# Layer 1 attention: where the exponentials' sums are added, and when the product with ones follows

## The chip, the cores and the metric

The kernel runs on one core of a Trainium2 chip. The metric is the time of one execution on the device, in microseconds (us). All data is 32-bit floating point.

## The reference

Four batches of 1024 rows of x (512 features) pass through two layers of cross attention against a context of 1024 rows (384 features). Layer 0 has 16 heads of 64 features, a layer norm ahead of it and its own weights. Layer 1, the one that is changed, has 16 heads of 32 features. Cut to what matters:

```python
xn = x * rsqrt(mean(x * x) + EPS_RMS) * norm_w
q = (xn @ wq).reshape(B, 1024, 16, 32)
k, v = split((context @ wkv).reshape(B, 1024, 2, 16, 32))
q, k = rotate(q), rotate(k)                 # rotary embedding
q, k = q / norm(q), k / norm(k)             # over each head
attn = softmax(einsum("bqhd,bkhd->bhqk", q, k) * sqrt(32))
out = x + einsum("bhqk,bkhd->bqhd", attn, v).reshape(B, 1024, 512) @ wout
```

The softmax needs, for each query and head, the sum over 1024 keys of the exponentials. The kernel divides by it after the product with v.

## The kernel before

The batches run one after the other. Within a batch layer 0 goes through eight pairs of heads (`Attention0`), then layer 1 through two halves of its heads (`Attention1`): `half` 0 and 1, eight heads each, in two groups `g` of four heads.

A **block** of layer 1 is one `(half, g, qb)`: four heads (`j`) and 256 queries (`WQ`). A half has 8 blocks, all batches together 64. A block takes four **steps** `kk`, each of two tiles `c` of 128 keys, so a half has 32 steps, numbered `n` from 0, and `kk` is `n % 4`. One `step` issues:

- the scores: 8 calls (L577), keys in the partitions, queries along the row, into two tiles `s` of two PSUM banks each;
- two exponentials on ScalarE (L587) into `e`, which has one place for even and one for odd steps;
- `finish`: the division of an earlier block (`quotient`) if one is pending, then `product` of the step before: 8 calls (L616) that add v times the exponentials into the tile `av`, in bank f0;
- `fill`: as many queued items of other work as the remaining steps share out by their written costs;
- on VectorE two additions (L593), which put the step's two key tiles together into `both[:, kk]`, and for `kk` 1 and 2 one more (L597), which adds `both[:, kk]` to `both[:, 0]`.

After the last product of a block come the sums over the partitions: 4 calls with a tile of ones over `both[:, 0]` and 4 over `both[:, 3]` (L627), into the second half of `av`. Each call shows as two instructions in the profile. One ScalarE copy (L631) takes `av` to SBUF, and a step later VectorE forms the reciprocal (L634) and the product with it (L635), which gives the output tile `o`.

Within layer 1, all other PSUM tiles come from `bank`, which goes round f1, f2, f3; f0 is kept for `av`. In layer 0 it goes round f0 to f3. An item that begins a new tile takes the next bank and has to wait until the tile that had it before was read.

The queue of other work (`Units`) is a list written out by hand. In half 0 it holds chains of projections for q and k (`rotated_chains`: a projection, a square on ScalarE at L476 and three VectorE reads of the bank at L478 to L480, work on GpSimd at L485, L167, L489, and two chains later the transposes at L499), the values (`value_chains`), and four transposes for the norm (L245). The order within it, by `weave`, in short: projection of a chain, then the transposes of the chain two before. In half 1 it holds the output product of half 0 (`add_units`, evacuated by VectorE at L293) and the preparation of the next batch. In the last batch's half 1 (the *final* half) there are only output products; the blocks are sorted by `g`, so that a finished group of heads can be multiplied early. The output products of the last two groups are handed to the queue at fixed steps: 18, and 22, 26, 30.

At a batch's end `finish` and `quotient` are called at once, and layer 0 of the next batch begins. The tiles `both` and `rest` (which holds `avs` and half of the values) have the tag "big"; layer 0's `eT` take over these two buffers.

## Time and profile before

| | |
|---|---|
| median of 3 runs | 2955.73 us (2946.95 to 2957.67) |
| profiled execution, its own time | 2957.42 us |
| its span, first to last instruction | 2955.4 us |
| mean granted TensorE clock | 0.992 |
| TensorE (PE) busy | 2865.9 us, 97% |
| VectorE (DVE) busy | 2185.6 us, 74% |
| ScalarE (ACT) busy | 1436.6 us, 49% |
| GpSimd (POOL) busy | 935.9 us, 32% |
| L627, product with ones | 1024 instructions, 81.3 us busy |
| L593, additions of key tiles | 512, 701 ns each |
| L597, additions of steps | 128, 1248 ns each |
| L631, copy of `av` | 64, 587 ns each |
| L634 and L635, division | 64 each, 1748 and 498 ns |

How to read it: a share is busy time over the whole span, and busy times of PE overlap, because matmuls are pipelined: an instruction of 379 ns can follow another after 54. What an instruction adds to the path is read from the chain of waits, not from its duration. PEld is the loading of weights. In a group's line the number after the second bar is the idle time of the engine just before these instructions, and what ended it. A waiting time belongs to the last of several conditions. The timeline's columns are start, duration, engine, line, operation, tiles, shapes, and in brackets the idle time before.

### The profile page before, as it was taken

To read this page: it belongs to the slowest core of one execution; us is meant where nothing else is said; L and a number is where in the kernel's file an instruction comes from. 1 tells how busy PE (TensorE), PEld (TensorE's weight loads), DVE (VectorE), ACT (ScalarE), POOL (GpSimd) and SP (SyncE) were. 2 spreads that over 40 slices of the span, in tenths; PEclk is the share of its full clock that TensorE was granted. 3 is DMA by queue.
4 is the path that set the end of the run, shared out by engine and by line. 5 is a ranking of instruction groups with operands and counts; after the bars stand their busy time and mean duration, and the time that the engine had idled before them with its cause. 6 is when DMAs were issued, how large, how long until landed. Compare 5 with 4: busy or idle time off the path is not lost.

```text
span 2955.4 us, 66614 instructions
## 1 busy us (share of the span) xinstructions
PE 2865.9 (97%) x27336; PEld 1433.0 (48%) x27336; DVE 2185.6 (74%) x2952; ACT 1436.6 (49%) x2265; POOL 935.9 (32%) x776
## 2 busy tenths in 40 slices
PE   8999999999989999999998999999999999999998
PEld 4444445555444454555544444455554444445544
DVE  5677785877767778587776777868877677786787
ACT  4444444656434443466643444346664344444664
POOL 2343353320234335332023433534102343353310
PEclk9999999999999999999999999999999999999999
DMA  5878774010487877401048787730105887763000
GB/s 141 197 180 188 169 173 104 22 36 25 105 199 176 186 163 164 104 22 36 25 115 189 179 187 170 162 94 22 36 25 126 192 182 178 172 162 85 2 2 30
DMA packets 177552, 348.86 MB, mean 118 GB/s; under 512 B 37600, under 2 KB 93152, under 8 KB 177248
## 3 DMA queue, kind: packets, MB, share of 16 engines
q1 hardware_dynamic: 175920, 343.96, 49.5%
q8 instruction: 215, 3.52, 0.5%
q14 instruction: 89, 0.73, 0.1%
q10 hardware_dynamic: 1328, 0.66, 0.1%
HBM read 67.64 MB, written 8.39 MB: 26 GB/s over the span
## 4 chain that ended last, share of the span: by engine, by line
PE 80%; DVE 10%; SPq 4%; DMA 2%; issue 2%; ACT 1%; POOL 1%; DVEq 0%; ACTq 0%
PE s L365 15%; PE av L426 13%; PE po L163 10%; PE s L577 8%; PE pqT L163 7%; PE pv L163 7%; PE av L616 6%; PE pkT L163 6%; SPq L410 4%; PE q_p L163 3%; PE av L627 2%; DVE both L593 2%; DVE m L390 2%; PE k_p L163 1%; DMA wo<-in_Wo_dram 1%
## 5 line engine op out<-in xcount | busy, mean ns | idle before, releaser
L390 DVE TENSOR_REDUCE m<-s 128x1 f32<-128x1024 f32 x512 | 603.0, 1220 | 401.6 <-PE s L365 401.6
L587 ACT ACTIVATE e<-s 128x1024 f32<-128x1024 f32 x512 | 497.1, 1023 | 313.2 <-PE s L577 304.7
L391 ACT ACTIVATE e<-s,m 128x1024 f32<-128x1024 f32 x256 | 283.4, 1112 | 502.9 <-DVE m L390 240.7
L396 POOL TENSOR_SCALAR raw<-raw,li 128x1024 f32<-128x1024 f32 x256 | 286.4, 1119 | 734.2 <-DVE li L395 725.8
L365 PE MATMUL s<-qk 64*128 64x512 f32 x2048 | 518.1, 621 | 0.7 <-ACT qk L135 0.7
L391 ACT ACTIVATE raw<-s,m 128x1024 f32<-128x1024 f32 x256 | 285.9, 1117 | 470.0 <-DVE m L390 470.0
L426 PE MATMUL av<-eT,v 128*64 128x256 f32 x4096 | 470.4, 382 | 5.3 <-DMA eT<-e 2.3
L396 POOL TENSOR_SCALAR e<-e,li 128x1024 f32<-128x1024 f32 x256 | 286.3, 1119 | 493.8 <-DMA eT<-e 239.4
L593 DVE TENSOR_TENSOR both<-e 128x512 f32<-128x512 f32 x512 | 341.9, 701 | 116.1 <-ACT e L587 88.9
L426 PEld LDWEIGHTS av<-eT,v 128*64 128x64 f32 x4096 | 287.4, 137 | 225.2 <-issue 84.5
L365 PEld LDWEIGHTS s<-qk 64*128 64x128 f32 x2048 | 180.9, 188 | 283.9 <-issue 174.3
L577 PE MATMUL s<-q,k 32*128 32x256 f32 x4096 | 306.0, 401 | 5.9 <-ACT q L504 2.7
L399 DVE STREAM_TRANSPOSE e<-e 128x1024 f32<-128x1024 f32 x256 | 310.1, 1229 | 0.2
L399 DVE STREAM_TRANSPOSE e<-raw 128x1024 f32<-128x1024 f32 x256 | 310.0, 1229 | 0.0
L163 PE MATMUL po<-wo,vals 128*64 128x512 f32 x1024 | 242.7, 608 | 26.5 <-DMA wo<-in_Wo_dram 26.5
L577 PEld LDWEIGHTS s<-q,k 32*128 32x128 f32 x4096 | 192.2, 184 | 153.0 <-ACT e L587 72.1
L163 PE MATMUL pqT<-hT,w 128*64 128x512 f32 (+1 forms) x1216 | 240.7, 595 | 2.5 <-ACT hT L247 2.5
L293 DVE TENSOR_TENSOR x<-x,po 128x512 f32<-128x512 f32 x200 | 131.7, 679 | 112.2 <-PE po L163 112.2
L163 PEld LDWEIGHTS pv<-w,cT 128*64 128x64 f32 (+1 forms) x3360 | 170.3, 132 | 41.6 <-issue 34.8
L163 PE MATMUL pv<-w,cT 128*64 128x128 f32 (+1 forms) x3360 | 184.3, 274 | 0.7 <-ACT hT L247 0.7
L163 PE MATMUL pkT<-cT,w 128*64 128x512 f32 (+1 forms) x912 | 183.1, 597 | 0.0
L597 DVE TENSOR_TENSOR both<-both 128x1024 f32<-128x1024 f32 x128 | 159.7, 1248 | 4.4
(81 smaller groups left out, 2793.1 us busy)
## 6 DMA issues: line engine op xcount, KB each, us to landing
eT<-e SPq DMA_DIRECT2D x2048, 128.0 KB, 2.4
xr<-in_x_dram SPq DMA_DIRECT2D x32, 256.0 KB, 3.6
x<-in_x_dram SPq DMA_DIRECT2D x32, 256.0 KB, 4.6
wo<-in_Wo_dram SPq DMA_DIRECT2D x16, 512.0 KB, 4.4
out_dram<-x SPq DMA_DIRECT2D x32, 256.0 KB, 2.6
w<-in_Wq_dram SPq DMA_DIRECT2D x31, 256.0 KB, 3.1
c<-in_ctx_dram SPq DMA_DIRECT2D x32, 192.0 KB, 3.9
wkv<-in_wkv_dram SPq DMA_DIRECT2D x16, 384.0 KB, 3.4
```

The source lines that it names most:

```text
L163: nc.tensor.matmul(o[rr], lhsT[:, rr], rhs, start=start, stop=stop)
L365: nc.tensor.matmul(sc[j][:, kb * 512 : (kb + 1) * 512], pr["qT"][r[j], i * P : (i + 1) * P], pr["kT"][r[j], kb * 512 : (kb + 1) * 512], st ...
L390: nc.vector.tensor_reduce(m[:, j : j + 1], sc[j], AX.X, ALU.max, negate=True)
L391: nc.scalar.activation(e[j], sc[j].rearrange("p (g s) -> p g s", g=4), AF.Exp, bias=m[:, j : j + 1], accum_out=l[:, j : j + 1])
L396: nc.gpsimd.tensor_scalar(e[j], e[j], li[:, j : j + 1], HD0**-0.5, ALU.mult, ALU.mult)
L399: self.turn = [lambda j=j: nc.vector.transpose(self.e[:, :, i % BQ * 2 + j, :], e[j]) for j in range(2)]
L426: nc.tensor.matmul(av[r[j], :W].rearrange("p (t a i) -> p t a i", t=BQ, a=4), pr["v"][:, k, r[j]], eT[:, j, :, :, k * 32 : (k + 1) * 32], ...
L577: nc.tensor.matmul(sc[j // 2][:, j % 2, c, :], kT[rr, g, k * P : (k + 1) * P], qT[rr, g, qb * WQ : (qb + 1) * WQ], start=True, stop=True,)
L587: nc.scalar.activation(e, sc[u], AF.Exp, scale=float(np.sqrt(np.float32(HD1))))
L593: nc.vector.tensor_add(self.both[:, kk, 2 * u : 2 * u + 2, :], es[u][:, :, 0, :], es[u][:, :, 1, :])
L597: nc.vector.tensor_add(self.both[:, 0], self.both[:, 0], self.both[:, kk])
L616: nc.tensor.matmul(self.av[rr, 0, :], v[g][:, 2 * kk + c, rr], es[j // 2][:, j % 2, c, :], start=first and c == 0, stop=end and c == 1,)
```

## The change

`both` is used differently: places 0 and 1 are running sums `acc` for odd and even blocks, place 2 takes steps 1 and 2, place 3 the last step. The additions on VectorE stay as many. After a block's last product, the tile `av`, now half as wide, is copied at once; GpSimd adds `both[:, 3]` to `acc`; and the ones go over `acc` only, with 4 calls into a tile from `bank`, two steps after the last product with v (in the final half one step), ahead of that step's own product. A second copy takes the sums to SBUF, and the division follows one step later. At the end of batches 0 to 2 the three remaining calls of `finish` become items of the queue, ahead of the next batch's layer 0; in the last batch they follow at once. The output products of the last group are queued at steps 23, 27 and 31.

```diff
@@ Attention1.__init__
-            self.quotient = None
+            self.after = None
+            self.n = 0
+            self.hurry = False
@@ step
+            self.n += kk == 0
...
             self.finish()
-            self.last = (half, g, qb, kk, v, es, o)
+            self.last = (half, g, qb, kk, v, es, o, self.n % 2)
             self.u.fill(us)
+            acc, end = self.both[:, self.n % 2], self.both[:, 3]
+            into = acc if kk == 0 else end if kk == NT // 2 - 1 else self.both[:, 2]
             for u in range(2):
-                nc.vector.tensor_add(
-                    self.both[:, kk, 2 * u : 2 * u + 2, :], es[u][:, :, 0, :], es[u][:, :, 1, :]
-                )
+                nc.vector.tensor_add(into[:, 2 * u : 2 * u + 2, :], es[u][:, :, 0, :], es[u][:, :, 1, :])
             if 0 < kk < NT // 2 - 1:
-                nc.vector.tensor_add(self.both[:, 0], self.both[:, 0], self.both[:, kk])
+                nc.vector.tensor_add(acc, acc, into)
@@ finish
-            if self.quotient is not None:
-                self.quotient()
-                self.quotient = None
+            if self.after is not None:
+                self.after = self.after()
@@ product
-                self.av = ps_f.tile([P, 2, WQ], F32, tag="f0", name=f"av1_{n}")
+                self.av = ps_f.tile([P, WQ], F32, tag="f0", name=f"av1_{n}")
...
             if end:
-                for i in (0, NT // 2 - 1):
-                    for j in range(4):
-                        rr = slice(j * HD1, (j + 1) * HD1)
-                        nc.tensor.matmul(
-                            self.av[rr, 1, :], ones, self.both[:, i, j], start=i == 0, stop=i > 0
-                        )
-                s = self.avs[:, qb % 2]
-                nc.scalar.copy(s, self.av)
-                def divide(): ...
-                self.quotient = divide
+                s = self.avs[:, par]
+                nc.scalar.copy(s[:, 0, :], self.av)
+                acc = self.both[:, par]
+                nc.gpsimd.tensor_add(acc, acc, self.both[:, 3])
+                def sums():
+                    pp = bank(f"sum1_{n}")
+                    for j in range(4):
+                        rr = slice(j * HD1, (j + 1) * HD1)
+                        nc.tensor.matmul(pp[rr, :WQ], ones, acc[:, j], start=True, stop=True)
+                    nc.scalar.copy(s[:, 1, :], pp[:, :WQ])
+                    def divide(): ...          # the two VectorE instructions as before
+                    return divide
+                self.after = sums if self.hurry else lambda: sums
@@ the loop over batches
+            att1.hurry = final
...
-                    if final and n in (22, 26, 30):
-                        work.add(flat(adds[1][(n - 22) // 2 : (n - 18) // 2]))
+                    if final and n in (23, 27, 31):
+                        work.add(flat(adds[1][(n - 23) // 2 : (n - 19) // 2]))
...
         att1.finish()
-        att1.quotient()
+        if b == B - 1:
+            att1.finish()
+            att1.finish()
+        else:
+            work.add([(c, att1.finish) for c in (0.0, 0.25, 0.0)])
```

More of the change, by code (lines that the diff above doesn't have):

```diff
@@ L607, in product @@
         def product(self):
-            half, g, qb, kk, v, es, o = self.last
+            half, g, qb, kk, v, es, o, par = self.last
             n = f"{self.b}_{half}_{g}_{qb}"
             if kk == 0:
-                self.av = ps_f.tile([P, 2, WQ], F32, tag="f0", name=f"av1_{n}")
+                self.av = ps_f.tile([P, WQ], F32, tag="f0", name=f"av1_{n}")
             first, end = kk == 0, kk == NT // 2 - 1
@@ L616, in product @@
                     nc.tensor.matmul(
-                        self.av[rr, 0, :],
+                        self.av[rr, :],
                         v[g][:, 2 * kk + c, rr],
@@ L623, in product, with divide @@
             if end:
-                for i in (0, NT // 2 - 1):
+                s = self.avs[:, par]
[4 more added lines that the diff above has]
+                    pp = bank(f"sum1_{n}")
                     for j in range(4):
                         rr = slice(j * HD1, (j + 1) * HD1)
-                        nc.tensor.matmul(
-                            self.av[rr, 1, :], ones, self.both[:, i, j], start=i == 0, stop=i > 0
-                        )
-                s = self.avs[:, qb % 2]
-                nc.scalar.copy(s, self.av)
-                def divide():
-                    nc.vector.reciprocal(s[:, 1, :], s[:, 1, :])
-                    nc.vector.tensor_mul(o[g][:, qb * WQ : (qb + 1) * WQ], s[:, 0, :], s[:, 1, :])
-                self.quotient = divide
+                        nc.tensor.matmul(pp[rr, :WQ], ones, acc[:, j], start=True, stop=True)
+                    nc.scalar.copy(s[:, 1, :], pp[:, :WQ])
+                    def divide():
+                        nc.vector.reciprocal(s[:, 1, :], s[:, 1, :])
+                        nc.vector.tensor_mul(o[g][:, qb * WQ : (qb + 1) * WQ], s[:, 0, :], s[:, 1, :])
+                    return divide
+                self.after = sums if self.hurry else lambda: sums
             self.last = None
```

## The prediction

> **What bounds the kernel now.** I read the engine shares first, then the page's chain of waits by engine, then busy times by stretch.

> ```profile
> PE 2865.9 (97%) x27336; PEld 1433.0 (48%) x27336; DVE 2185.6 (74%) x2952; ACT 1436.6 (49%) x2265; POOL 935.9 (32%) x776
> ...
> PE 80%; DVE 10%; SPq 4%; DMA 2%; issue 2%; ACT 1%; POOL 1%; DVEq 0%; ACTq 0%
> ```

> TensorE is busy nearly throughout. For layer 1, the busy times of three stretches (PE, PEld, DVE, ACT, POOL): batch 0's half 0, its half 1, and the final half of batch 3.

> ```profile
> 494.00:627.00 133.00, 126.26 (x1918) 69.93 (x1920) 102.97 (x144) 83.08 (x111) 46.80 (x29) 0.99 0.06 17
> 627.00:754.00 127.00, 126.72 (x1786) 65.14 (x1788) 92.61 (x129) 81.14 (x99) 3.07 (x4) 1.00 0.11 35
> 2834.00:2941.00 107.00, 104.07 (x1359) 50.46 (x1352) 86.66 (x113) 66.05 (x72) 0.00 (x0) 1.00 0.03 9
> ```

> PE is the bound here too; half 0 loses 6.7 us of 133. The chain of waits inside half 1 shows one step and prices its parts:

> ```profile
> 642.93 1.08 PE s L577 x16
> 644.01 1.00 PE av L616 x16
> 645.01 0.86 PE av L627 x16
> 645.88 1.72 PE po L163 x16
> ```

> A step is scores (1.08), product with v (1.00), then queued work; on the first step of a block the 16 ones instructions (L627, two for each call) add 0.86 us, 53.75 ns each. Groups by form and PE's list of waits say what else L627 costs:

> ```profile
> L627 PE MATMUL av<-both,ones 128*32 128x256 f32 x1024 | 81.3, 382 | 15.4 <-DVE both L593 15.4
> ```
> ```profile
> PE av L627 <- DVE both L593: 15.4, 9, 2.2
> ...
> PE pth L245 <- DVE rot L480: 6.7, 4, 1.7
> ...
> PE q_t L499 <- POOL rot L489: 2.3, 4, 0.6
> ```

> The first wait is PE standing still for VectorE's last add. The second recurs once per batch and shows what a short bank rotation costs; the timeline of its place:

> ```profile
> 519.77 0.61 PE L163 MATMUL k_p<-wkv,cT 128*32 128x256 f32 x8
> ...
> 520.32 1.09 PE L245 MATMUL pth<-ident,xn 128*128 128x128 f32 x8
> ...
> 520.81 0.61 ACT L476 ACTIVATE rot<-k_p 128x512 f32<-128x512 f32 x1
> ...
> 521.58 0.68 DVE L478 TENSOR_TENSOR rot<-k_p,cos 128x512 f32<-128x512 f32 x1
> ...
> 522.51 0.42 DVE L480 TENSOR_TENSOR rot<-k_p,sin 128x256 f32<-128x256 f32 x1
> ...
> 523.07 0.63 PE L245 MATMUL pth<-ident,xn 128*128 128x128 f32 x4 [1.66 <-DVE rot L480]
> ```

> A projection ends at 520.3; two transposes take the other two banks; the third needs the projection's bank and waits until ScalarE's square and three VectorE reads are over, 2.7 us after the projection's end. At 586.8 the same series took 2.6 us, at 534.8 2.2 us.

> [...]

> ```profile
> 549.92 1.05 POOL L489 TENSOR_TENSOR rot<-rot,k_r 128x512 f32<-128x512 f32 x1
> ...
> 550.19 1.06 DVE L635 TENSOR_TENSOR o<-rest 128x256 f32<-128x256 f32 x1
> ```

> L635 takes 0.42 elsewhere. Beneath the power L167 (3.2 us) an L597 kept its 1.23[...]. [...] L478 above begins only after the square has ended. [...] L616 and L627 share 128*32 and follow without a gap; the moved ones stand right before a product, in the same mode.

> **The change, part by part.**

> *Removed.* Of each block's 8 ones calls 4 go: 8 instructions x 53.75 ns x 64 blocks = **27.5 us** of PE on the path. The wait for L593 loses its place: 15.4 less 0.3 of the very last block = **15.1 us**. Together 42.6.

> *GpSimd's add.* 128x1024 with two inputs is not in the trace; the nearest row is

> ```profile
> L282 POOL TENSOR_TENSOR x<-x,bo x32: 1260/1265/1274, 143.3 to 2407.2; 128x512 f32<-128x512 f32 x32
> ```

> Twice that is 2.53 us (estimate). [...] I take 2.53. It starts when the last L593 ends and the ones follow two steps (about 7.5 us) later, so PE should not wait. VectorE may: 0 to 2.53 us a block, 0 to 162 us in all. Between a block's last add and the next block's first one VectorE often has 1 to 2 us without a two-input add, so I take 1.3, which its 23% of free time in half 0 covers. GpSimd has 86 us free of 133; its own queue holds the rotations, which feed transposes two chains later.

> *Copies.* Two 128x256 copies (373 ns, row L135) for one 128x512 (587): 0.16 x 64 = 10 us of ScalarE, which is under two thirds busy. Hidden; if that cover is gone, 10 us at most. Reciprocal and multiplication move to a step without L597: nothing, since only the output products need them, many steps later.

> *The bank.* The old ones used the product's own bank f0. The new ones take the next of f1 to f3, so each block turns the rotation of three by one. I wrote down which bank every queue item of half 0 takes, step by step (the queue follows from the written costs; its items per step match the trace: 4, 3, 1+2, 4, ...). New short reuses in each batch: at step 6 the second transpose, not the third, gets the projection's bank: +0.6. At step 18 the ones wait for the bank of q1's first projection: released 4.9 us after step 17 begins, wanted at 4.6: 0.3. At step 22 q1's third projection follows the second in the same bank with only a transpose (0.59) between; release 2.6, less what the extra ones before it shift: 1.8. At step 27 the second-half values follow q1's last projection likewise; release 2.5 to 4.1 (4.1 at 606 to 610, where VectorE is late): 2.2. At step 4 the q transposes already wait 0.56 for GpSimd's rotation; coming 0.86 earlier they wait 0.86 more. At steps 10 and 15, with 2.5 to 3 us between, 0.5.

> Sum 6.3 us a batch, **25 us** in four. Bounds: 0 (if releases come early) and 2.6 at each of six places, 62 us. Half 1 has longer intervals, evacuated mostly by ScalarE: 0.7 x 3 = 2 us (0 to 8).

> *The final half.* Ones wait one step only. PE there sometimes waits for L587 already, so up to 0.86 a block could be won; but VectorE has 86.7 of 107 us busy and gets 8 locks. I take a loss of 1.4 against the sum above (-4 to +8). The output products, moved from steps 22, 26, 30 to 23, 27, 31, keep a full step after their division: 0.

> *The ends.* Batch 3's last sum: L593, then 2.53 on GpSimd, half the ones, a shorter copy: +2.3 us with nothing beside it. Other batches' last ones run between 64-column products of the next batch[...]. The buffers that the next layer 0 takes over are read in its first queued items, before its first regroup; no new DMA or SP step is issued.

> Sum: -42.6 + 25 + 2 + 1.4 + 2.3 + 1 = about **-11 us**. The profiled execution took 2957.42 us (span 2955.4), 1.7 above the runs' median 2955.73. So 2957.4 - 10.7 = 2946.7 on its terms, **2945** on the median's.

> **Rivals.** A, *the banks cost nothing*: releases come before they are asked for, as VectorE is relieved in a block's second step. Then -42.6 + 2.3 + 1 = -39: 2917. For it: no bank wait in half 1's PE list. Against: the wait at 523.07, and two places with 0.59 us between.

> B, *slower: the lock becomes backlog at the bank releases of half 0*. From 560 to 627 VectorE has 54.3 us busy; four whole locks (10.1) make 64.4 of 67. If at three places a batch a whole 2.53 is still unworked when the rotation's reads are due, 4 x 3 x 2.53 = 30: -11 + 30 = +19, 2975. It decides once backlog outlasts the two steps between the add and the next tight place. For it: L593 in fours (back to back, two steps late). Against: the idle time after L597 on other steps.

> C, *the ones do not move*: GpSimd starts late behind a rotation (4.9 us of queue) and PE waits at the ones as before: 27.5 saved, 15 kept, banks paid, near 2956.

> **How the numbers follow.** My forecast 0.50, A 0.25, B 0.18, C 0.07. About 0.5%, 15 us, is what a measurement of this kernel can tell from no change. My forecast's own range, 2932 to 2957, puts 0.3 of its chance below 2940.9; with A that is 0.40 for faster. B's upper part gives 0.14 slower, 0.46 remain. The range 2915 to 2966 takes in A and the lower half of B.

> **What would show it.** L627 with 512 instructions and some 27 us; no wait of L627 for L593; new PE waits for L480 at a projection and at values in half 0, near 2 us each, four times each; GpSimd adds of 2.5 us; single L593 of up to 3 us; two copies of 373 ns. Wrong, if half 0 has no new bank waits (A), or if PE waits for GpSimd's add or L587 for L593 in half 0 (B, C).

## The result, and the profile after

The changed kernel takes **2989.26 us** (median of 4 runs, 2982.83 to 2991.30) against 2951.94 for the kernel before on the same chip (4 runs, 2946.95 to 2957.67): ratio 1.0122, interval 1.0095 to 1.0149. It is slower by 37 us, where 2945 (2915 to 2966) was forecast. The profiled execution has a span of 2989.5 us, before 2955.4: 34.1 more. The mean granted TensorE clock went from 0.992 to 0.982. Numbers of lines moved with the change: exponentials L590, additions of key tiles L599, of steps L601, scores L580, product with v L619, copy of `av` L628, GpSimd's addition L631, ones L637, copy of the sums L638, division L641 and L642.

From the page after: engine shares, chain of waits by engine, and two groups (busy us, mean ns of one | idle time ahead and what ended it).

```profile
PE 2853.3 (95%) x26824; PEld 1427.7 (48%) x26824; DVE 2254.1 (75%) x2952; ACT 1435.4 (48%) x2329; POOL 1097.1 (37%) x840
...
PE 73%; DVE 14%; SPq 5%; DMA 3%; issue 2%; POOL 2%; ACT 2%; POOLq 0%; DVEq 0%; ACTq 0%
...
L599 DVE TENSOR_TENSOR both<-e 128x512 f32<-128x512 f32 x512 | 394.0, 809 | 86.3 <-ACT e L590 84.2
...
L631 POOL TENSOR_TENSOR both<-both 128x1024 f32<-128x1024 f32 x64 | 158.4, 2475 | 398.9 <-DVE both L599 342.1
```

TensorE lost seven points of the chain of waits (80% before), and VectorE gained four (10% before). VectorE has as many instructions as before, but 68.5 us more busy time; 52 of them are in L599, 809 ns each where L593 took 701.

The groups by form after show what replaced the wait of the ones for L593 (15.4 us before):

```profile
L637 PE MATMUL sum<-both,ones 128*32 128x256 f32 x512 | 43.1, 410 | 36.2 <-POOL both L631 27.6 <-DVE rot L480 8.6
...
L590 ACT ACTIVATE e<-s 128x1024 f32<-128x1024 f32 x512 | 496.7, 1023 | 335.3 <-PE s L580 295.7 <-DVE both L599 24.7 <-issue 13.1
```

There are half as many ones and no wait for L599, but PE stands still 27.6 us for GpSimd's addition and 8.6 for a bank. The exponentials now wait 24.7 us for additions (2.2 before), which free their tiles `e` late.

Busy times by stretch after (length; PE, PEld, DVE, ACT, POOL with instructions; granted clock; DMA share; GB/s), the same three stages that the forecast shows of before:

```profile
497.00:639.00 142.00, 127.02 (x1876) 70.98 (x1872) 111.04 (x143) 83.54 (x118) 65.83 (x37) 0.94 0.05 14
639.00:763.00 124.00, 121.94 (x1672) 62.29 (x1668) 100.00 (x128) 79.59 (x104) 21.95 (x12) 0.99 0.12 36
2864.00:2971.00 107.00, 98.88 (x1300) 48.28 (x1288) 98.26 (x113) 66.05 (x80) 19.40 (x8) 1.00 0.02 7
```

In half 0, PE idles 15 us of 142 (before 6.7 of 133), at a clock of 0.94. The lengths of all stages follow. Half 0 runs from its first exponentials to the first output product of half 1, half 1 from there to layer 0's first scores, layer 0 to the next first exponentials, and the final half to the end. Differences are of the unrounded times.

| us | before | after | difference, all batches |
|---|---|---|---|
| half 0, four batches | 133.7, 132.1, 132.1, 132.1 | 141.8, 140.4, 142.1, 142.1 | +36.3 |
| half 1, three batches | 124.1 each | 124.4, 122.8, 122.8 | -2.5 |
| final half to the end | 120.5 | 125.2 | +4.8 |
| layer 0, three batches | 480.2, 478.4, 477.8 | 475.8, 478.9, 475.9 | -5.8 |

With 1.4 at the start these make the 34.1. The loss is in half 0, in every batch alike. PE's waits after (total us, times, longest us), the lines that the change touches:

```profile
PE sum L637 <- POOL both L631: 27.6, 11, 4.3
...
PE pv L163 <- DVE rot L480: 13.6, 4, 3.4
PE sum L637 <- DVE rot L480: 8.6, 4, 2.2
...
PE pth L245 <- DVE rot L480: 7.3, 4, 1.8
PE q_p L163 <- DVE rot L480: 7.3, 4, 1.8
...
PE q_t L499 <- POOL rot L489: 5.7, 4, 1.4
```

The five waits below it recur once in each batch, at places that the forecast named (steps 27, 18, 6, 22 and 4); GpSimd's addition heads the list. The timeline after shows the place of the longest wait (start us, us, engine, line; in brackets the idle time ahead):

```profile
546.08 1.75 DVE L641 RECIPROCAL rest<-rest 128x256 f32<-128x256 f32 x1
...
547.85 0.43 DVE L642 TENSOR_TENSOR o<-rest 128x256 f32<-128x256 f32 x1
...
548.20 0.68 DVE L478 TENSOR_TENSOR rot<-k_p,cos 128x512 f32<-128x512 f32 x1
...
550.78 3.71 DVE L599 TENSOR_TENSOR both<-e 128x512 f32<-128x512 f32 x6
...
550.95 0.62 POOL L485 TENSOR_SCALAR k_m<-k_s 128x16 f32<-128x16 f32 x1 [3.89 <-DVE k_s L483]
...
551.58 1.94 ACT L590 ACTIVATE e<-s 128x1024 f32<-128x1024 f32 x2 [2.21 <-DVE both L599]
551.66 3.20 POOL L167 TENSOR_TENSOR k_r<-k_m,nhalf 128x16 f32<-128x16 f32 x1
...
554.93 1.73 POOL L489 TENSOR_TENSOR rot<-rot,k_r 128x512 f32<-128x512 f32 x1
556.63 2.33 POOL L631 TENSOR_TENSOR both<-both 128x1024 f32<-128x1024 f32 x1
559.01 1.08 PE L637 MATMUL sum<-both,ones 128*32 128x256 f32 x8 [4.31 <-POOL both L631]
```

Read from the top. The division (2.1 us) stands in VectorE's queue ahead of a rotation's bank reads. So these, and three steps' L599, are late: six run back to back. ScalarE waits for them. GpSimd receives the rotation late too, and the addition, which is issued behind L485, L167 and L489, starts only when they have ended, at 556.63. PE waits 4.31 us.

The same timeline further on shows the other half of the mechanism, the bank that the values ask for at step 27:

```profile
616.79 1.75 DVE L641 RECIPROCAL rest<-rest 128x256 f32<-128x256 f32 x1
616.85 0.60 ACT L476 ACTIVATE rot<-q_p 128x512 f32<-128x512 f32 x1
...
618.92 0.68 DVE L478 TENSOR_TENSOR rot<-q_p,cos 128x512 f32<-128x512 f32 x1
...
620.41 0.64 PE L163 MATMUL pv<-wkv,cT 128*32 128x256 f32 x8 [3.40 <-DVE rot L480]
```

ScalarE's square ends at 617.45, but L478 starts 1.5 us later, after the division. Last, the clock around the first place (stretch after; the granted clock is the third number from the end):

```profile
555.00:559.00 4.00, 0.00 (x0) 0.00 (x0) 0.76 (x1) 1.29 (x2) 3.96 (x2) 0.64 0.00 0
559.00:561.00 2.00, 1.99 (x20) 0.99 (x24) 0.00 (x0) 0.37 (x1) 0.00 (x0) 0.50 0.00 0
...
563.00:565.00 2.00, 2.00 (x32) 1.24 (x28) 0.98 (x3) 1.13 (x2) 0.00 (x0) 1.00 0.14 30
```

PE's work after the wait runs at half clock until about 563: the ones take 1.08 us there, 0.64 at 578.07.

This is not the only such place. In the four halves 0 the granted clock is 0.50 for 64.9 us, before for 3.4. The next lines show step 6, before and then after, where the transposes of the norm wait for a bank, 1.66 and 1.82 us:

```profile
520.25:523.66 3.41, 1.75 (x20) 1.31 (x16) 3.34 (x7) 2.32 (x4) 0.00 (x0) 1.00 0.00 0
523.66:527.08 3.42, 3.42 (x53) 1.94 (x52) 3.39 (x5) 2.96 (x4) 2.66 (x2) 1.00 0.00 0
```
```profile
521.99:525.40 3.41, 1.59 (x17) 1.23 (x12) 3.28 (x6) 1.78 (x5) 0.00 (x0) 1.00 0.00 0
525.40:528.81 3.41, 3.41 (x31) 1.86 (x33) 3.38 (x5) 2.11 (x4) 2.84 (x2) 0.50 0.00 0
```

The clock of these traces changes only on a grid of 3.41 us (in before and after every change lies within 0.01 us of it). What tells the two apart is how long PE was busy in the grid stretch just before: 1.75 us kept full clock here, 1.59 lost it. Over all 14 traces of this case, a stretch at full clock with PE busy for under 40% of it was followed by half clock in 141 of 141 cases, one with 40 to 50% in 43 of 79, one with more in 2 of 11,600; in before and after alone in 20 of 20, 10 of 14 and 1 of 1,654.

### The profile page after: what moved, and what is told of

Read it like the earlier page. It is cut to its first block, busy times and chain, and to the rows that moved or that the text cites. A ratio compares the mean times of both kernels' runs of the same rounds, so it can differ in the third digit from the quotient of the medians.

```text
span 2989.5 us, 65785 instructions
## 1 busy us (share of the span) xinstructions
PE 2853.3 (95%) x26824; PEld 1427.7 (48%) x26824; DVE 2254.1 (75%) x2952; ACT 1435.4 (48%) x2329; POOL 1097.1 (37%) x840
## 4 chain that ended last, share of the span: by engine, by line
PE 73%; DVE 14%; SPq 5%; DMA 3%; issue 2%; POOL 2%; ACT 2%; POOLq 0%; DVEq 0%; ACTq 0%
PE s L365 14%; PE av L426 13%; PE po L163 9%; PE s L580 7%; PE pv L163 6%; PE pqT L163 6%; PE av L619 6%; PE pkT L163 5%; SPq L410 4%; DVE both L599 3%; PE q_p L163 3%; PE k_p L163 2%; DVE m L390 2%; DVE both L601 1%; DVE rest L641 1%
## 5 line engine op out<-in xcount | busy, mean ns | idle before, releaser
L590 ACT ACTIVATE e<-s 128x1024 f32<-128x1024 f32 x512 | 496.7, 1023 | 335.3 <-PE s L580 295.7
L599 DVE TENSOR_TENSOR both<-e 128x512 f32<-128x512 f32 x512 | 394.0, 809 | 86.3 <-ACT e L590 84.2
L580 PE MATMUL s<-q,k 32*128 32x256 f32 x4096 | 316.3, 410 | 3.7 <-ACT q L504 2.7
L631 POOL TENSOR_TENSOR both<-both 128x1024 f32<-128x1024 f32 x64 | 158.4, 2475 | 398.9 <-DVE both L599 342.1
L580 PEld LDWEIGHTS s<-q,k 32*128 32x128 f32 x4096 | 198.7, 188 | 150.9 <-ACT e L590 71.8
L163 PE MATMUL po<-wo,vals 128*64 128x512 f32 x1024 | 244.9, 612 | 17.2 <-DMA wo<-in_Wo_dram 17.1
L163 PE MATMUL pqT<-hT,w 128*64 128x512 f32 (+1 forms) x1216 | 240.6, 595 | 2.4 <-ACT hT L247 2.4
L293 DVE TENSOR_TENSOR x<-x,po 128x512 f32<-128x512 f32 x200 | 131.7, 677 | 91.8 <-PE po L163 91.8
L163 PEld LDWEIGHTS pv<-w,cT 128*64 128x64 f32 (+1 forms) x3360 | 170.5, 132 | 39.1 <-issue 32.9
L163 PE MATMUL pv<-w,cT 128*64 128x128 f32 (+1 forms) x3360 | 184.3, 274 | 0.7 <-ACT hT L247 0.7
L163 PE MATMUL pkT<-cT,w 128*64 128x512 f32 (+1 forms) x912 | 183.5, 599 | 0.0
```

What stands on the lines that cost most here:

```text
L163: nc.tensor.matmul(o[rr], lhsT[:, rr], rhs, start=start, stop=stop)
L580: nc.tensor.matmul(sc[j // 2][:, j % 2, c, :], kT[rr, g, k * P : (k + 1) * P], qT[rr, g, qb * WQ : (qb + 1) * WQ], start=True, stop=True,)
L590: nc.scalar.activation(e, sc[u], AF.Exp, scale=float(np.sqrt(np.float32(HD1))))
L599: nc.vector.tensor_add(into[:, 2 * u : 2 * u + 2, :], es[u][:, :, 0, :], es[u][:, :, 1, :])
L631: nc.gpsimd.tensor_add(acc, acc, self.both[:, 3])
```

## The experiments

Three causes were to be told apart: the turn of the bank rotation, GpSimd's addition (its late end, or its lock on VectorE: additions there that take longer while it runs, on the mean of the changed kernel 809 ns against 701), and the division's place. Each ratio is against runs of the kernel before on the same chip (medians 2951.55 to 2954.38).

**The turn alone, from both sides.** r_bank takes it out of the changed kernel: the ones still take the next bank, but the rotation does not move on.

```diff
+                    turn = which["n"]
                     pp = bank(f"sum1_{n}")
+                    which["n"] = turn
```

> The changed kernel, but the ones take a bank without turning the rotation: the next item takes the same bank again, so all other items keep the banks that they had before the change. Bank theory (the new waits for L480 and L293, 37 us of PE's list, cost the time): these waits fall back to the 7 us that the kernel before had, and the time to 2989 - 30 to 40 = 2950 to 2959. GpSimd theory (the waits for GpSimd's late addition and the lower clock after them cost it): the 27.6 us of waits for L631 stay; if they are all, the time stays above 2980. Lock theory (VectorE is late because it is locked out): L599 stays near 809 ns, time above 2980.

r_skip puts it into the kernel before, with nothing else:

```diff
+            self.blk = getattr(self, "blk", -1) + (kk == 0)
+            if kk == 2 and self.blk:      # from the second block on
+                which["n"] = which["n"] + 1 if which["n"] < 3 else which["from"]
             self.finish()
```

> The kernel before, but the bank rotation is turned by one on the third step of each block from the second on, with no tile in the bank that is passed over: only the numbering of the banks is that of the changed kernel. Bank theory: PE gets new waits for L480, near 2 us at a projection and 2 to 3.5 us at the values in half 0, 5 to 9 us a batch, so 20 to 36 us more: 2972 to 2988. If banks are not it: 2952, no new wait of PE over 1 us for L480.

r_bank: 3010.09, ratio 1.0198 (1.0181 to 1.0215). r_skip: 2973.04, ratio 1.0082 (1.0062 to 1.0102). PE's waits in r_bank:

```profile
PE sum L639 <- POOL both L631: 45.3, 15, 4.8
...
PE pv L163 <- ACT rest L640: 10.1, 3, 3.4
```

Taking the turn out did not help in all, and neither expectation had 3010. The next item now asks for the ones' own bank and waits for its copy on ScalarE (L640). Half 0 still became 5.8 us shorter over four batches: the waits at steps 6, 22 and 27 went, and longer waits for GpSimd took part of their place. But half 1 grew by 5.5 and layer 0 by 23.2; the three waits of 3.4 shown stand where layer 0 begins. So r_bank says little about the turn. r_skip does: without any other part of the change it costs 21 us, nearly all in half 0, which takes 138 to 140 us. Its PE waits:

```profile
PE pv L163 <- DVE rot L480: 14.0, 4, 3.5
PE pth L245 <- DVE rot L480: 8.4, 4, 2.1
...
PE q_p L163 <- DVE rot L480: 7.9, 4, 2.0
```

These are steps 27, 6 and 22, in sizes like those of the changed kernel. They are 23.6 us more than before, but they are not the whole account: the ones' waits for additions shrink from 15.4 to 6.5, and half 0 has 34.1 us at half clock (before 3.4).

**The addition alone, beside the kernel before.** r_dummy lets GpSimd add `both[:, 3]` into an unused place once a block. r_memset lets it fill that place with zeros three times instead: about as long, but nothing is read.

```diff
+            self.spare = rest[:, 1]...      # the unused place, filled once a batch
...
                 nc.scalar.copy(s, self.av)
+                nc.gpsimd.tensor_add(self.spare, self.spare, self.both[:, 3])   # r_dummy
+                for _ in range(3):                                              # r_memset
+                    nc.gpsimd.memset(self.spare, 0.0)
```

> The kernel before, plus one GpSimd addition of 128x1024 for each block into a spare tile that nobody reads, queued at the place where the changed kernel has its own and waiting for the same last L593 (and one memset for each batch). No bank is turned, and PE waits for none of it. Lock theory: L593 rises from 701 towards 809 ns and VectorE's lateness makes PE wait longer for L593 than 15 us: 10 to 40 us more, 2962 to 2992. Bank theory, or GpSimd theory in which only PE's own wait for the addition counts: within 5 us of 2952, L593 longer but hidden.

> The kernel before with three GpSimd memsets of 128x1024 (0.95 us each, about 2.9 us) for each block into the spare tile, in place of the one addition of r_dummy: GpSimd's queue is as long taken, but nothing is read from SBUF. Lock theory for the 17 us of r_dummy: 2952, within 4, L593 at 701 ns as before. Queue theory (GpSimd's rotations come later): 2960 to 2970 as in r_dummy.

r_dummy: 2968.61, ratio 1.0056 (1.0041 to 1.0071). r_memset: 2969.44, ratio 1.0058 (1.0042 to 1.0074). The fill (968 ns each) reads nothing, and VectorE's additions kept 700 ns (774 in r_dummy), yet it costs the same. So the lock on additions isn't what these 17 us are. The timelines of r_memset and, second, of before at the norm of the first batch:

```profile
516.39 3.29 POOL L635 MEMSET rest<- 128x1024 f32 x3
...
516.48 3.87 DVE L234 TENSOR_SCALAR xn<-x,rs 128x512 f32<-128x512 f32 x4 [2.85 <-POOL rs L167]
...
527.55 1.08 PE L245 MATMUL pth<-ident,xn 128*128 128x128 f32 x4 [3.85 <-DVE rot L480]
```
```profile
514.20 1.67 DVE L234 TENSOR_SCALAR xn<-x,rs 128x512 f32<-128x512 f32 x4 [2.85 <-POOL rs L167]
```

GpSimd's instruction follows directly on L167, which releases L234. The four L234 then take 3.87 us, where they took 1.67; a rotation's reads behind them are late, and the transposes of the norm wait 3.85 us for its bank (1.66 before) and then take 1.08 us for four, in place of 0.63. So L234, a tensor-by-scalar operation, takes longer beside a fill, and about as long beside r_dummy's addition (3.76 us), while the additions of two tiles kept 700 ns on the mean beside the fills. The forecast reckoned with the additions alone. In the changed kernel these L234 take 3.76 us too, but the division, which had followed them, now stands elsewhere, and the wait is the 1.82 of step 6.

**GpSimd's addition out of the changed kernel.** r_eight lets the ones go over both places again, at the changed places in the order. r_dve gives the addition to VectorE.

```diff
-                nc.gpsimd.tensor_add(acc, acc, self.both[:, 3])
+                nc.vector.tensor_add(acc, acc, self.both[:, 3])          # r_dve only
...
-                        nc.tensor.matmul(pp[rr, :WQ], ones, acc[:, j], start=True, stop=True)
+                        nc.tensor.matmul(pp[rr, :WQ], ones, acc[:, j], start=True, stop=False)   # r_eight only
+                    for j in range(4):
+                        ... over both[:, 3], start=False, stop=True
```

> The changed kernel without GpSimd's addition: the ones go over both tiles of sums, eight calls, at the same place two steps later and in a bank from the rotation. PE gets 27.5 us of work back. GpSimd theory: waits for L631 (27.6 us) and the lower clock after them (some 8 us) vanish, L599 falls back to about 700 ns: 2989 + 27 - 36 = 2980 or less. Bank theory: waits for L480 stay near 37 us, 3000 or more, since the added work is paid in full. Lock theory: VectorE is no longer late, so the bank waits shrink as well: below 2970.

> The changed kernel with the last addition of a block on VectorE instead of GpSimd (1.23 us x 64 = 79 us more on VectorE; no lock, no place in GpSimd's queue). Banks turn as in the changed kernel, and four ones calls stay removed. If it is the lock and GpSimd's queue that cost: near the version with eight ones calls less their 27 us, so 2925 to 2940. If VectorE's total work in half 0 (103 us of 133 before, 113 with this) limits: 2955 to 2985.

r_eight: 2954.50, ratio 1.0006 (1.0000 to 1.0013). r_dve: 2952.48, ratio 1.0002 (0.9994 to 1.0011). Two groups of r_dve:

```profile
L599 DVE TENSOR_TENSOR both<-e 128x512 f32<-128x512 f32 x512 | 341.8, 699 | 82.1 <-ACT e L590 79.9
...
L631 DVE TENSOR_TENSOR both<-both 128x1024 f32<-128x1024 f32 x64 | 78.4, 1225 | 2.2
```

On VectorE the addition takes 1.23 us, half of GpSimd's 2.48, and L599 fall back to 699 ns. Although VectorE does 78.4 us more, the kernel is 37 us faster than the changed one; at 2952 it lies between the two ranges that were expected. r_eight does 27 us more on PE and is 35 us faster. Moving the addition to GpSimd as this change does thus costs more than either alternative. How much of that is the lock and how much the queue that the addition stands in, these two don't tell: both take away both. Both keep the division early and the turned banks, and the waits for L480 with them (13.6 us at step 27 in r_dve, as in the changed kernel); so these alone don't make the 37 us.

**The order in time.** r_three keeps every part of the change but gives the ones and the division one step more (halves other than the final one).

```diff
-                self.after = sums if self.hurry else lambda: sums
+                self.after = sums if self.hurry else lambda: lambda: sums
...
-            work.add([(c, att1.finish) for c in (0.0, 0.25, 0.0)])
+            work.add([(c, att1.finish) for c in (0.0, 0.0, 0.25, 0.0)])
```

> The changed kernel with the ones three steps behind the last product instead of two (in the final half one, as it is). Theory that PE's wait for GpSimd's late addition (4.3 us once in each half 0) and the halved TensorE clock after it (2.1 us more) are a large part: both vanish there, 4 x 6.4 = 26 us less, about 2963; banks still turn. Rival, that VectorE's lateness is the limit and PE's wait only the place where it shows: the time moves to waits of the exponentials for L599 and of PE for L480, and stays above 2980.

r_div leaves the ones where the change put them and issues the division at its step's end, behind the queued work's reads and the additions.

```diff
+            held = None
+            if kk == (2 if self.hurry else 3):
+                held, self.after = self.after, None
             self.finish()
...
+            if held is not None:
+                held()
```

> The changed kernel with the division (L641, L642) issued at the end of its step, behind the additions, instead of at its begin. Theory that the division, which the change moved onto the block's last step ahead of a rotation's reads and the last addition, is what makes VectorE and with it GpSimd late: the wait of 4.3 for GpSimd falls to about 2 and keeps the clock, the wait of 3.4 at the values falls to about 1.5: 4 x (2.2 + 2 + 2.2 + 1) = 30 less, about 2960. Rival, that the lock alone makes it late: above 2980.

r_late8 is the kernel before, with all eight ones and their place in f0, but issued after the queued work of the next block's first step; the running sums alternate between two places.

```diff
             self.u.fill(us)
+            if self.ones is not None:
+                self.ones()
```

> The kernel before with all eight ones calls in their own bank f0, issued at the end of the same step, after the queued work instead of before it (running sums in places 0 and 1 in turn, so that VectorE need not wait). No bank is turned, GpSimd does nothing. Theory that the waits for L593 (15 us) and the lower clock after some of them can be had alone: 2952 - 15 to 25 = 2927 to 2937. Rival, that VectorE's lateness comes up at the next wait: 2945 to 2952.

r_three: 2929.17, ratio 0.9922 (0.9907 to 0.9937). r_div: 2966.00, ratio 1.0050 (1.0033 to 1.0068). r_late8: 2929.13, ratio 0.9924 (0.9908 to 0.9941). PE's waits in r_three:

```profile
PE sum L637 <- POOL both L631: 10.3, 7, 3.6
...
PE pv L163 <- DVE rot L480: 9.3, 4, 2.3
```

All seven waits for GpSimd are in the final half, where nothing was moved. Half 0 has 127.0 to 128.6 us, half 1 120.8 in every batch. With one step more, the change brings 23 us instead of costing 37. That is 60 us of difference, where 26 were expected of the wait and the clock after it; the addition is still on GpSimd, and L599 take 755 ns. r_div shows the weight of the division's place: half 0, at 133.3 to 133.8 us, is 32.6 shorter over four batches than in the changed kernel and half 1 5.2 over three, while the final half grew by 8.1, to 133.3. r_late8 brings as much as r_three with no GpSimd work, no other bank and no instruction less. Its ones hardly wait for an addition any more (1.8 us in place of 15.4), and its half 0 has no stretch at half clock; how the rest of its 23 us divides stays open.

**One at a time between the changed kernel and r_three.** r_div4 moves only the division, by one step; r_turn2 moves division and ones, but takes the bank as early as the change does.

```diff
-                    return divide
+                    return divide if self.hurry else lambda: divide      # r_div4
...
+                def take():                                              # r_turn2
+                    got.append(bank(f"sum1_{n}"))
+                    return sums
...
-                self.after = sums if self.hurry else lambda: sums
+                self.after = sums if self.hurry else lambda: take
```

> The changed kernel with the ones three steps behind, as r_three, but their bank is taken from the rotation one step earlier, at the place where the changed kernel takes it; so the banks turn as in the changed kernel, and only the ones, their copy and the division are a step later. Bank theory: the waits for L480 at a projection (1.8) and at the values stay, 2929 + 4 x 3 = 2940 to 2948. If the wait for GpSimd and what follows it were the whole of the difference to r_three: 2929, within 5.

> The changed kernel with only the division (L641, L642) one step later, at the begin of the next block's first step, outside the final half; the ones stay two steps behind and their bank is taken where the changed kernel takes it. Theory that the place of the division, ahead of a rotation's reads and of the block's last addition, makes VectorE late: half 0 falls from 141 us to 133 or less a batch, the exposed wait for GpSimd from 4.3 to 3 or less and without a lower clock after it, the wait at the values from 3.4 to 2; 2989 - 4 x 8.5 = 2955, and what is left to r_turn2 (2946) is the wait for GpSimd at the ones. Rival, that the ones' step alone counts: above 2980.

r_turn2: 2946.10, ratio 0.9970 (0.9956 to 0.9985). r_div4: 2964.67, ratio 1.0029 (1.0018 to 1.0041). The series of medians:

| kernel | median | what is moved against the row above |
|---|---|---|
| changed | 2989.26 | |
| r_div4 | 2964.67, -24.6 | the division a step later |
| r_turn2 | 2946.10, -18.6 | the ones a step later |
| r_three | 2929.17, -16.9 | their bank taken a step later, and so held a step less |

By the ratios the three are 27, 17 and 14 us; the chips differ a little (the kernel before took 2951.77 to 2954.38 on them). The amounts hold for this order of steps, with GpSimd's addition in the kernel. PE's waits in r_div4:

```profile
PE sum L637 <- POOL both L631: 25.8, 15, 3.6
PE pv L163 <- DVE rot L480: 7.9, 4, 2.0
...
PE sum L637 <- DVE rot L480: 4.9, 4, 1.2
```

With the division away, PE waits 1.4 us less for the bank at step 27 (2.0 against 3.4) and 0.9 less at step 18; at the place of the 4.31 it waits 3.06. In the profiled executions half 0 is 27 us shorter over four batches, and PE's idle time makes only 11 of them. The other 16 are in PE's busy time, with the same instructions. The granted clock goes with them: half 0 has 27.3 us at half clock in r_div4, 64.9 in the changed kernel. So more than half of what the division's place costs in half 0 seems to come through the clock. VectorE's queue still shows the lock:

```profile
552.23 5.49 DVE L599 TENSOR_TENSOR both<-e 128x512 f32<-128x512 f32 x4
...
554.39 2.79 POOL L631 TENSOR_TENSOR both<-both 128x1024 f32<-128x1024 f32 x1
```

Four additions take 5.49 us, where two took 1.28 at 548.91: some 2.9 more, beside one GpSimd addition and the L489 ahead of it (1.36 us from 553.06).

**A version that uses it.** r_best is r_three, with the final half as r_eight has it (eight ones, no GpSimd addition, one step behind).

```diff
-                nc.gpsimd.tensor_add(acc, acc, self.both[:, 3])
+                both = not self.hurry
+                if both:
+                    nc.gpsimd.tensor_add(acc, acc, self.both[:, 3])
...
+                    # in the final half four more ones over both[:, 3], as in r_eight
```

> r_three with the final half changed: there no GpSimd addition, but eight ones calls over both tiles, one step behind. If the final half loses by its waits for GpSimd (10.3 us) and VectorE's lock: its 124.3 us fall to near the 117.0 of the run with eight calls, so 2929 - 7 = 2922, faster than both kernels by 1% and 2%. If PE's added 3.4 us eat it: 2929.

r_best: 2921.44, ratio 0.9895 (0.9880 to 0.9909): 32 us faster than before and 68 than the changed kernel. Its final half has 117.9 us (after 125.2, before 120.5).

## Why the prediction was wrong

*What was right.* The price of the ones: in half 1 r_three is 3.3 us shorter than before, forecast 8 x 0.43 = 3.4. The wait for L593 is gone. The addition takes 2.48 us (2.53). The bank turn has about the price that the list of banks gave: r_skip shows 21 us for it alone (25 to 27 forecast), so rival A falls. That the sums agree is in part luck: in r_skip shorter waits for additions and more half clock, neither of them in the list, nearly balance. At the end, first L599 to reciprocal takes 5.38 us against 2.63 before, +2.75 (2.3 forecast).

*"So PE should not wait".* This step failed. It reckoned GpSimd's addition from the last addition on VectorE, and set two steps, 7.5 us, against 2.5 of duration. But the addition stands in two queues: VectorE's, where the last L599 is late, and GpSimd's own, behind a rotation of 5.6 us (0.62, 3.20 and 1.73). Measured are 27.6 us of waiting, 17.3 in half 0 and 10.3 in the final half. Rival C had named this queue, with a chance of 0.07. Its own number, 2956, left out what comes with it, and also the final half and the ends of the forecast's own sum, which would have made it 2960.

*"Reciprocal and multiplication move to a step without L597: nothing".* This step failed too, and in the order of the table above it is the dearest: 25 to 27 us. It asked who needs the division's result, and not what stands behind the division in VectorE's queue. Where it stands now, a rotation's bank reads follow it at 548.20 and 618.92. Before, it stood after a rotation, with additions behind it:

```profile
545.17 0.68 DVE L483 TENSOR_REDUCE k_s<-rot 128x16 f32<-128x512 f32 x1
...
548.40 1.75 DVE L634 RECIPROCAL rest<-rest 128x256 f32<-128x256 f32 x1
...
551.54 0.69 DVE L593 TENSOR_TENSOR both<-e 128x512 f32<-128x512 f32 x1 [0.29 <-ACT e L587]
```

The new place is rival B's, the bank releases, with the division in the part that B gave to the lock; B's price of 30 us came close to the 36.3 of half 0 for a reason only partly its own.

*The lock.* 1.3 us a block were taken, the author's estimate; the one case shown for it was L635 (1.06 us beside L489, 0.42 elsewhere). VectorE's busy time grew by 52 us in L599, 0.81 a block. The size was taken too large rather than too small, but the cover was wrong: "its 23% of free time in half 0" is a mean, and at 550.78 there was none.

*The banks' sizes.* Per batch, forecast and measured: step 6 0.6 and 0.16; step 18 0.3 and 2.16; step 22 1.8 and 1.82; step 27 2.2 and 3.40; step 4 0.86 and 0.87; steps 10 and 15 0.5 and 0. In half 0 6.3 became 8.4. Two of these sizes depend on how late VectorE is: without the division ahead of them, step 27 has 2.0 and step 18 1.2 (r_div4). But r_skip has 3.5 at step 27, with the division elsewhere and other additions late ahead of the reads; the forecast had 2.5 to 4.1 as bounds of that release and took the low end. In half 1, at its step 18, 1.8 in place of 0.7.

*What was left out.* The clock, which the forecast put at nothing. The traces show it halved mostly after a stretch of the grid in which PE was busy for under about half of the 3.41 us, and a wait of 1.82 us at step 6 (PE busy for 1.59 us) cost full clock where one of 1.66 (1.75) had not. It depends on how a wait lies in these stretches. In r_div4 the 3.06 us at one place fell mostly into one stretch in two batches (PE busy for 22 and 26% of it), and ones of 1.08 us followed; in the other two they were shared by two stretches (48 to 62% in each), and ones of 0.64 us followed.

*The sum.* Half 0 should have changed by -3.4 for the ones, -3.8 for the waits on L593 (a quarter of 15.1) and +6.3 for banks, -0.9 a batch. It changed by +9.1. Of these 10.0, GpSimd's waits make 4.3 and larger bank waits 2.1: PE's idle time rose from 6.1 to 15.0 (by the bounds of the table of stages), where the forecast had 2.5 more. The other 3.6 are in PE's busy time, which should have fallen by the 3.4 of the ones and rose by 0.2. The half clock is more than enough for them: 13.7 to 17.1 us a batch at 0.50 could cost 6.9 on the mean (an estimate, half of PE's busy time in these stretches). The final half was to change by -2.0 and +2.3 at its end; it changed by +4.8, with 10.3 us of waits for GpSimd in it, where VectorE has 98.3 us busy of 107 (86.7 before). The forecast's 1 us for the other batches' last ones was the author's estimate; no run shows it.

*What stays open.* How lock and queue divide GpSimd's part. No run changes the clock alone, so its share is read from PE's busy time. Layer 0, which the change hardly touches, took 474 to 487 us over all kernels; its -5.8 here goes with shorter waits for the weights `wo` (17.1 us against 26.5) and less time at half clock (27.3 us against 37.5), but why these changed isn't shown.

## What to carry to other kernels

A moved instruction is priced by what stands behind it in its engine's queue, not only by who needs its result: here two VectorE instructions that nothing waited for cost 25 us ahead of three bank reads, with GpSimd's addition in the kernel. Work put on an idle engine comes at the end of that engine's queue (here behind a rotation of 5.6 us), so its consumer needs the queue's length as distance, not the instruction's; one step more, for the ones, their bank and the division, turned this change from 37 us lost to 23 won. But r_late8 won as much by a later place alone, with nothing moved to another engine. A new tile in a rotation of three banks lets the items behind it ask for a used bank one turn sooner (21 us in r_skip), and where it enters is worth trying. And a short wait of TensorE can cost more than its length: after one of 1.82 us here the granted clock was 0.50 for 3.41 us.
